# An attention result divided with its features on partitions, its row sums moved by DMA

## The chip, the cores and the metric

The kernel runs on one core of a Trainium2 chip. The core has five engines that run their own instruction streams in order: TensorE (PE in the profile; its weight loads are listed apart as PEld), VectorE (DVE), ScalarE (ACT), GpSimd (POOL) and SyncE (SP), which here only starts transfers. Engines wait for one another through semaphores. SBUF is the on-chip memory with 128 partitions; PSUM is the small memory that TensorE writes its products to.

The metric is the device time of one execution in microseconds (us). Lower is better. Before the change it was 1411.76 us, the median of three runs from 1406.98 to 1413.27.

## The reference

The kernel computes one decoder layer with post-normalisation, all in float32, on `x` of shape (16, 512, 256):

```
q = x@wq + 4*(x@Aq)@Bq ;  k = x@wk ;  v = x@wv + 4*(x@Av)@Bv      # 16 heads of 16 features
q, k = rope(q), rope(k)
a = softmax(causal(q k^T / 4)) @ v                                 # per head, 512 x 512 scores
x1 = layernorm(x + a @ wo)                                         # no scale, no shift
h  = gelu(butterfly_up(x1 @ W_exp + b_exp) + up_bias)              # 1024 hidden features
y  = layernorm(x1 + butterfly_down(h) @ W_con + b_con + down_bias)
```

A butterfly is ten stages of 2x2 mixes between features whose numbers differ in one bit. It is linear, so the kernel folds both butterflies into the two weight matrices at run time, on the chip, during the first batches.

## The kernel before

There are 16 batches (`B`) of 512 tokens, 4 token tiles of 128 (`NT`), 256 features in 2 chunks of 128 (`NC`), and 1024 hidden features in 8 chunks (`NHC`).

**Attention.** Scores are computed with keys on partitions, so the softmax can't take a row maximum along the free axis. Each batch is therefore gone through twice. `largest` computes q k^T with queries on partitions, and VectorE reduces each product to the row maximum (line 427); `place_largest` transposes these and puts them into a spare row of q. `weights` computes the scores again, transposed, with the maximum already subtracted by that spare row; ScalarE takes the exponential out of PSUM (line 487), and GpSimd zeroes the masked half of each diagonal block (line 491). `weigh` multiplies by v (line 514). The operand `vaug` holds 32 columns for each head, 16 of v and 16 of ones, so the 32 output rows of a head are 16 result features and 16 copies of the sum of the exponentials. Four heads fill the 128 partitions of the PSUM tile `po`: the even or the odd heads (`par`) of one chunk (`c`). One such pass, (b, c, par), is a quad here; a batch has four.

**Dividing and turning.** `normalize_heads` copies `po` to SBUF on ScalarE (line 529). `turn_back` transposes it on TensorE in four pieces, tokens to partitions (line 536); VectorE takes the reciprocals of the sums (line 539) and multiplies (line 541). When all four quads of a batch are done, `turn_heads` transposes each token tile back, features to partitions (line 552), ScalarE copies it out of PSUM (line 554), and `project_out` multiplies by `wo` (line 561), adds x on VectorE (line 565) and takes the statistics of the first layer norm (lines 575, 576).

**Behind it.** `spread` adds epsilon (line 587) and takes the power -1/2 on GpSimd (line 588). `offset` makes the shift on VectorE (line 593), `centre` applies both on ScalarE, one instruction for each token tile (line 600), and `turn_x1` transposes the normalised tile for the next product (line 614). `hidden` is the product with the folded up-weights (line 631), copied out of PSUM alternately by VectorE and ScalarE; `gelus` follows on ScalarE, `contract` is the product with the folded down-weights (line 658) in two halves for each token tile. Then come `spread`, `offset` and `centre` of the second layer norm and `store`.

**Order.** No scheduler reorders anything: the order of the program is the order on each engine. It is written as a loop over slots. A batch takes 20 slots (`per`), a quad 5 (`PER_QUAD`), and the `weights` pass runs 15 slots behind the `largest` pass (`behind`). In each slot come first the score products of both passes, then the work on them (exponentials, masks, the VectorE reductions), then the `weigh` step that is due, then the list `others[slot]`, then `holes[slot]`, then pieces of the folding of the weights. `add(s + n, f, ...)` puts a function into `others` of the slot n after the first slot s = 20 b of batch b. The lists are filled batch by batch, so within a slot the older batch's functions stand first. Since a batch's work reaches 64 slots past its start, a slot holds work of up to four batches. The prediction calls a slot by its number modulo 20: p4 is slot 4 of every twenty, and within a quad u0 to u4 are the slots modulo 5.

The score products of a slot go to two PSUM tiles, `pb` and `pa`, of which there is one each, so the products of a slot wait for the exponentials and reductions of the slot before. In u0 to u3 one of the two tiles belongs to `weights` and the other to `largest`; in u4 each holds half of both. All other products share a ring of three PSUM tiles.

## Time and profile before

| | |
|---|---|
| time, median of three runs | 1411.76 us (1406.98 to 1413.27) |
| the profiled execution | 1415.53 us, its span in the trace 1413.8 us |
| instructions | 24605 |
| VectorE, ScalarE, GpSimd busy | 59%, 51%, 36% of the span |
| DMA, mean over the span | 36 GB/s |
| transposes for dividing and turning | 256 of `oT`, 128 of `o` |
| `wo` products | 256 instructions |
| VectorE reductions of `largest` | 1024, with a read of the accumulator each |
| GpSimd masks | 512 |

Busy times of a group are the union of its instructions' times. TensorE's instructions overlap each other, so the sum of its groups is more than its busy time; the chain of work that ended last gives the share in which an instruction was not overlapped by the one before. A float32 product with moving data appears as two instructions in the trace and a transpose as one. In a list of instructions each line has the start, the duration, the engine, the line, the operation, output and input, and in brackets how long the engine had been idle before it and what ended that.

### The profile page before, as it was taken

How to read it: one execution, taken by the hardware profiler on the slowest of the kernel's cores; microseconds unless marked ns; L12 is line 12 of the kernel's file. 1: busy time of each engine (PE TensorE's matmuls, PEld its weight loads, DVE VectorE, ACT ScalarE, POOL GpSimd, SP SyncE). 2: the span in 40 equal slices, each digit the busy share in tenths (PEclk: the TensorE clock that was granted, in tenths of full speed). 3: DMA queues.
4: the chain of work that ended last, by engine and by line, in shares of the span. 5: the costliest groups of instructions: out<-in, count | busy, mean ns of one | idle time of the engine just before them, and what ended most of it. 6: DMA issues, size and time to landing. Idle time of an engine off the chain costs nothing.

```text
span 1413.8 us, 24605 instructions
## 1 busy us (share of the span) xinstructions
PE 1379.7 (98%) x9208; PEld 758.6 (54%) x9208; DVE 828.0 (59%) x2846; ACT 720.1 (51%) x1120; POOL 511.0 (36%) x779
## 2 busy tenths in 40 slices
PE   8899999999999999999999999999999999998998
PEld 4454546465564645555464555545455564644565
DVE  5766656556575655657465565746556574664422
ACT  2665455544555454555445455544545555445553
POOL 3534225253342425334252433514244252521311
PEclk9998999999999999999999999999999999999999
DMA  5310000100010010001101100010011001000000
GB/s 180 114 31 16 32 31 16 61 17 32 31 47 30 17 53 24 32 31 32 46 17 42 36 32 31 23 55 16 32 46 32 31 17 60 3 31 2 16 1 30
DMA packets 36472, 50.43 MB, mean 36 GB/s; under 512 B 3704, under 2 KB 23160, under 8 KB 36352
## 3 DMA queue, kind: packets, MB, share of 16 engines
q1 hardware_dynamic: 32464, 43.30, 8.8%
q10 hardware_dynamic: 3888, 5.55, 1.3%
q8 instruction: 73, 1.20, 0.3%
q14 instruction: 47, 0.39, 0.1%
HBM read 22.88 MB, written 8.39 MB: 22 GB/s over the span
## 4 chain that ended last, share of the span: by engine, by line
PE 94%; ACT 2%; DVE 2%; issue 1%; DMA 0%; POOLq 0%; POOL 0%; DVEq 0%; ACTq 0%
PE pb L470 20%; PE py L658 17%; PE ph L631 16%; PE po L514 11%; PE pqk L339 8%; PE pwo L561 4%; PE pvv L385 4%; PE pa L418 3%; PE pto L536 2%; PE pb L418 2%; DVE junk L427 1%; PE ptm L443 1%; PE pt L614 1%; PE ptc L552 1%; PE pd L269 1%; PE pa L470 1%
## 5 line engine op out<-in xcount | busy, mean ns | idle before, releaser
L427 DVE CUSTOM_DVE_ANT_0 junk<-pa,causal 128x384 bf16<-128x384 f32 (+2 forms) x878 | 439.3, 500 | 240.9 <-PE pa L418 209.5
L487 ACT ACTIVATE pT<-pb 128x1024 f32<-128x1024 f32 (+1 forms) x314 | 293.7, 935 | 365.4 <-PE pa L418 266.6
L491 POOL TENSOR_SCALAR_AFFINE_SELECT pT<-pT 128x256 f32<-128x256 f32 x512 | 202.5, 408 | 755.6 <-ACT pT L487 751.3
L470 PE MATMUL pb<-qz,kz 17*128 17x512 f32 (+2 forms) x1756 | 330.0, 475 | 10.7 <-ACT pT L487 9.9
L418 PE MATMUL pa<-kz,qz 32*128 32x384 f32 (+3 forms) x1756 | 324.6, 469 | 3.8 <-DVE mx L427 3.7
L658 PE MATMUL py<-wdn,h 128*128 128x256 f32 x1024 | 253.3, 392 | 1.4 <-ACT h L649 1.4
L631 PE MATMUL ph<-x1T,yb 128*128 128x512 f32 x512 | 236.1, 605 | 0.0
L470 PEld LDWEIGHTS pb<-qz,kz 17*128 17x128 f32 (+1 forms) x1756 | 142.3, 184 | 154.7 <-issue 92.7
L658 PEld LDWEIGHTS py<-wdn,h 128*128 128x128 f32 x1024 | 185.2, 190 | 69.6 <-issue 43.7
L514 PE MATMUL po<-pT,vaug 128*32 128x512 f32 (+3 forms) x2048 | 179.7, 446 | 0.0
L418 PEld LDWEIGHTS pa<-kz,qz 32*128 32x128 f32 (+1 forms) x1756 | 148.7, 185 | 18.5 <-DVE mx L427 9.9
L631 PEld LDWEIGHTS ph<-x1T,yb 128*128 128x128 f32 x512 | 92.4, 190 | 115.3 <-issue 101.7
L427 DVE CUSTOM_DVE_ANT_0 junk<-pb,causal 128x256 bf16<-128x256 f32 (+3 forms) x146 | 63.6, 435 | 111.2 <-ACT pT L487 102.2
L339 PE MATMUL pqk<-xT,wqk 128*128 128x512 f32 x256 | 119.4, 617 | 0.0
L644 ACT COPY h<-ph 128x512 f32<-128x512 f32 x57 | 33.4, 585 | 147.2 <-PE ph L631 147.2
L514 PEld LDWEIGHTS po<-pT,vaug 128*32 128x32 f32 x2048 | 47.4, 109 | 103.2 <-issue 89.4
L427 DVE DVE_READ_ACCUMULATOR2_ANT mx<- 128x1 f32 x1024 | 84.8, 83 | 0.0
L339 PEld LDWEIGHTS pqk<-xT,wqk 128*128 128x128 f32 x256 | 48.6, 197 | 67.1 <-issue 55.2
L600 ACT ACTIVATE z<-z,norm 128x256 f32<-128x256 f32 x128 | 66.9, 590 | 27.6 <-DVE norm L593 27.6
L367 POOL TENSOR_TENSOR swap<-swap,rope_sb 128x512 f32<-128x512 f32 x62 | 79.8, 1287 | 0.0
L588 POOL TENSOR_TENSOR norm<-norm,power 128x4 f32<-128x4 f32 (+1 forms) x38 | 35.0, 922 | 113.7 <-DVE norm L587 111.7
L649 ACT ACTIVATE h<-h,hbias 128x512 f32<-128x512 f32 x115 | 72.0, 708 | 0.2
(96 smaller groups left out, 1419.4 us busy)
## 6 DMA issues: line engine op xcount, KB each, us to landing
xT<-in_xT SPq DMA_DIRECT2D x16, 512.0 KB
swap<-qz SPq DMA_DIRECT2D x64, 128.0 KB
swap<-kz SPq DMA_DIRECT2D x64, 128.0 KB
z<-in_x SPq DMA_DIRECT2D x16, 512.0 KB
out_y<-z SPq DMA_DIRECT2D x15, 512.0 KB
early<-in_wexpT ACTq DMA_DIRECT2D x1, 1028.0 KB
wdn<-in_wcon ACTq DMA_DIRECT2D x1, 1024.0 KB
qz<-mT SPq DMA_DIRECT2D x64, 8.0 KB
```

The lines of the kernel that those rows point to most:

```text
L339: nc.tensor.matmul(pq, wqk[:, d, e : e + P], xTs[b][:, d, :], start=(d == 0), stop=(d == NC - 1))
L367: engine.tensor_tensor(swap, swap, rope_sb[:, 1, :], ALU.mult)
L418: lambda i=i, rows=rows, at=at, n=n, t=t, ps=ps: nc.tensor.matmul(ps[:, i, at : at + n], q[rows, par, t * P : n], k_[rows, par, 0:n], star ...
L427: lambda i=i, at=at, n=n, t=t, col=col, ps=ps: nc.vector.tensor_tensor_reduce(out=junk[:, 0:n], in0=ps[:, i, at : at + n], in1=causal[:, T ...
L470: lambda i=i, rows=rows, at=at, n=n, k=block, ps=ps: nc.tensor.matmul(ps[:, i, at : at + n], kt[rows, par, k * P : (k + 1) * P], qt[rows, ...
L487: nc.scalar.activation(pT[:, heads, 0:n], ps[:, :, at : at + n], AF.Exp)
L491: nc.gpsimd.affine_select(out=diag, in_=diag, pattern=[[0, 2], [1, P]], compare_op=ALU.is_ge, fill=0.0, base=0, channel_multiplier=-1,)
L514: nc.tensor.matmul(po[HG * g : HG * (g + 1), k * P : T], vaugs[b % 2][:, k, h, :], pT[:, g, at : at + n], start=(k == 0), stop=(group == 2),)
L600: nc.scalar.activation(zs[b][:, t, :], zs[b][:, t, :], AF.Identity, bias=norm[:, 2, t : t + 1], scale=norm[:, 1, t : t + 1],)
L631: nc.tensor.matmul(ph, wup[:, c, hc * P : (hc + 1) * P], state["x1T", b][:, c, :], start=(c == 0), stop=(c == NC - 1),)
L649: nc.scalar.activation(h[:, hc, :], h[:, hc, :], AF.Gelu, bias=hbias[:, hc : hc + 1])
L658: nc.tensor.matmul(py, state["h", b][:, hc, t * P : (t + 1) * P], wdn[:, hc, :], start=(hc == 0), stop=(hc == NHC - 1),)
```

## The change

The result of `weigh` stays with features on partitions. `vaug` is laid out for each pair of heads with ones at every even column and the two heads' features, interleaved, at every odd one. Read from column 33 it gives v, 1, v, 1, ... for the even head, read from column 0 it gives 1, v, 1, v, ... for the odd head. So the even head's features land on even partitions with its sums on the odd ones, and the odd head's the other way round. `wv`, `Bv` and `wo` are permuted on the host to match. After the ScalarE copy to SBUF, transfers on SP's queue, of 64 partitions each, put the sums beside the features they belong to: for an even quad one transfer to `sums`, for an odd quad one to `sums` and one that drops its features between those of the even quad. `normalize` then takes, for each chunk and token tile, the reciprocal of 128x128 sums in place on VectorE and multiplies 128x128. `project_out` reads the result directly. `turn_back`, `turn_heads` and the copy of `ocT` are gone.

Four other things change. `project_out` and what follows it stand three slots later, and the slots of `project_v`, the projections, `load_x`, `hidden` and `contract` are set anew. The last stage of the up-butterfly runs as products with diagonal matrices on TensorE instead of multiply-adds on ScalarE and VectorE. VectorE copies two of the eight hidden chunks out of PSUM instead of four, and ScalarE the others. The fillings of `vaug` and `mx` stand at the start of the program.

```diff
--- before.py
+++ after.py
@@ -181,7 +181,7 @@
         qz.append([const.tile([P, 2, T], F32, name=f"qz{r}_{c}") for c in range(NC)])
         kz.append([const.tile([P, 2, T], F32, name=f"kz{r}_{c}") for c in range(NC)])
     for r in range(2):
-        vaugs.append(const.tile([P, NT, NH, HG], F32, name=f"vaug{r}"))
+        vaugs.append(const.tile([P, NT, NH // 2, 2 * HG + 2], F32, name=f"vaug{r}"))
     for c in range(NC):
         mxs.append(const.tile([P, NT, P], F32, name=f"mx{c}"))
 
@@ -189,11 +189,10 @@
 
         return ap.rearrange("(g i) t -> g i t", i=HG)[:, first : first + count, :]
 
-    def prepare_mx(c):
+    for r in range(2):
+        nc.gpsimd.memset(vaugs[r], 1.0)
+    for c in range(NC):
         nc.gpsimd.memset(mxs[c], 0.0)
-
-    def prepare_vaug(r):
-        nc.gpsimd.memset(vaugs[r][:, :, :, DH:HG], 1.0)
 
 
 
@@ -281,7 +280,7 @@
         for s in stages:
             for c in range(NHC):
                 if not c & (1 << (s - NSP)):
-                    by = across_by_products if side == 0 and s < NS - 1 else across_chunks
+                    by = across_by_products if side == 0 else across_chunks
                     yield by(side, s, c, y, cols)
 
     def mixed(one, two):
@@ -389,7 +388,12 @@
                 start=(d == 0),
                 stop=(d == NC - 1),
             )
-        nc.scalar.copy(vaugs[b % 2][:, t, :, 0:DH], pv.rearrange("p (h i) -> p h i", i=DH))
+        nc.scalar.copy(
+            vaugs[b % 2][:, t, :, 1 : 1 + 2 * HG].rearrange("p g (h i e) -> p g h i e", h=2, e=2)[
+                :, :, :, :, 0
+            ],
+            pv.rearrange("p (g h i) -> p g h i", h=2, i=DH),
+        )
 
 
 
@@ -510,10 +514,10 @@
         for k in GROUPS[group]:
             n = width(k)
             for g in range(NG):
-                h = 2 * NG * c + 2 * g + par
+                first = 0 if par else HG + 1
                 nc.tensor.matmul(
                     po[HG * g : HG * (g + 1), k * P : T],
-                    vaugs[b % 2][:, k, h, :],
+                    vaugs[b % 2][:, k, NG * c + g, first : first + HG],
                     pT[:, g, at : at + n],
                     start=(k == 0),
                     stop=(group == 2),
@@ -522,44 +526,39 @@
         if group == 2:
             normalize_heads(b, c, par, po)
 
+
+
+
+    def rows_of(ap, e):
+        return ap.rearrange("(i two) t -> i two t", two=2)[:, e, :]
+
     def normalize_heads(b, c, par, po):
-        if (c, par) == (0, 0):
-            state["o", b] = ring2.tile([P, NT, NH, DH], F32, tag="o", name=f"o_{b}", bufs=1)
-        oT = ring2.tile([P, T], F32, tag="oT", name=f"oT_{b}_{c}_{par}")
-        nc.scalar.copy(oT, po)
-        state["back", b, c, par] = oT
-
-    def turn_back(b, c, par):
-        oT = state.pop(("back", b, c, par))
-        pt = bank(f"pto_{b}_{c}_{par}", [P, NT, P])
-        for t in range(NT):
-            nc.tensor.transpose(pt[:, t, :], oT[:, t * P : (t + 1) * P], ident)
-        heads = pt.rearrange("p t (g i) -> p t g i", i=HG)
-        rec = small.tile([P, NT, NG, 1], F32, tag="rec", name=f"rec_{b}_{c}_{par}")
-        nc.vector.reciprocal(rec, heads[:, :, :, DH : DH + 1])
-        o = state["o", b].rearrange("p t (c g two) i -> p t c g two i", c=NC, two=2)
-        nc.vector.tensor_tensor(
-            o[:, :, c, :, par, :],
-            heads[:, :, :, 0:DH],
-            rec.to_broadcast([P, NT, NG, DH]),
-            ALU.mult,
-        )
-
-    def turn_heads(b, t):
-        of = state["o", b][:, t, :, :].rearrange("p h i -> p (h i)")
-        pc = bank(f"ptc_{b}_{t}", [P, NC, P])
-        for c in range(NC):
-            nc.tensor.transpose(pc[:, c, :], of[:, c * P : (c + 1) * P], ident)
-        ocT = small.tile([P, NC, P], F32, tag="ocT", name=f"ocT_{b}_{t}", bufs=4)
-        nc.scalar.copy(ocT, pc)
-        state["ocT", b, t] = ocT
+        x = ring2.tile([P, T], F32, tag=f"x{par}", name=f"x_{b}_{c}_{par}", bufs=1 if par else 3)
+        nc.scalar.copy(x, po)
+        if par == 0:
+            sums = ring2.tile([P, T], F32, tag="sums", name=f"sums_{b}_{c}")
+            state["heads", b, c] = x, sums
+            nc.sync.dma_start(rows_of(sums, 0), rows_of(x, 1))
+        else:
+            even, sums = state["heads", b, c]
+            nc.sync.dma_start(rows_of(sums, 1), rows_of(x, 0))
+            nc.sync.dma_start(rows_of(even, 1), rows_of(x, 1))
+
+    def normalize(b, c, t):
+        x, sums = state["heads", b, c]
+        ts = slice(t * P, (t + 1) * P)
+        nc.vector.reciprocal(sums[:, ts], sums[:, ts])
+        nc.vector.tensor_tensor(x[:, ts], x[:, ts], sums[:, ts], ALU.mult)
 
     def project_out(b, t):
-        ocT = state.pop(("ocT", b, t))
         pw = bank(f"pwo_{b}_{t}", [P, D])
         for c in range(NC):
             nc.tensor.matmul(
-                pw, ocT[:, c, :], wo_sb[:, c, :], start=(c == 0), stop=(c == NC - 1)
+                pw,
+                state["heads", b, c][0][:, t * P : (t + 1) * P],
+                wo_sb[:, c, :],
+                start=(c == 0),
+                stop=(c == NC - 1),
             )
         z = zs[b]
         nc.vector.tensor_add(z[:, t, :], pw, z[:, t, :])
@@ -638,7 +637,7 @@
         h = state["h", b][:, hc, :]
         if fused:
             nc.scalar.activation(h, ph, AF.Gelu, bias=hbias[:, hc : hc + 1])
-        elif hc % 2 == 0:
+        elif hc % 4 == 0:
             nc.vector.tensor_copy(h, ph)
         else:
             nc.scalar.copy(h, ph)
@@ -707,20 +706,17 @@
         add((-2, -1, 0, 0)[t], project_v, 0, t)
     for n, at in enumerate((-1, 4, 6, 9, 12)):
         add(at, load_more, n)
-    for i in range(2):
-        add(-head, prepare_mx, i)
-        add(4 + i, prepare_vaug, i)
     for b in range(B):
         s = b * per
         if b > 0:
 
-            at = {1: (-16, -11, -13, -9), B - 1: (-4, 7, 7, 11)}.get(b, (-4, -3, 14, 11))
+            at = {1: (-16, -11, -13, -9), B - 1: (-3, 10, 10, 11)}.get(b, (-3, 4, 11, 11))
             for t in range(NT):
                 add(s + at[t], project_v, b, t)
         if b + 1 < B:
 
             add(s - head * (b == 0), load_xT, b + 1)
-            at = {0: (2, 5, 7, 10), 1: (3, 6, 8, 11)}.get(b, (7, 7, 7, 7))
+            at = {0: (2, 5, 7, 10), 1: (3, 6, 8, 11)}.get(b, (10, 10, 10, 10))
             for i, (c, side) in enumerate(chains):
                 holes.setdefault(s + at[i], []).append(
                     lambda b=b, side=side, c=c: start_projection(b + 1, side, c)
@@ -729,40 +725,39 @@
                     add(s + max(at[0] + 1 + 3 * i, at[i] + 1) + step, turn, b + 1, side, c, step)
                 for step in range(1 + side):
                     add(s + max(at[0] + 1 + 3 * i, at[i] + 1) + 4 + step, part, b + 1, side, c, step)
-        add(s + 5, load_x, b)
+        add(s + 9, load_x, b)
         add(s + 11, place_largest, b, 0)
         add(s + 21, place_largest, b, 1)
-        for n in range(NQ):
-            at = s + behind + PER_QUAD * n + 6 + (b + 1 == B)
-            if at < end:
-                add(at, turn_back, b, n // 2, n % 2)
+        for c in range(NC if b + 1 < B else 1):
+            for t in range(NT):
+                at = s + ((26, 27, 28, 29), (36, 37, 38, 40))[c][t] + (b + 1 == B)
+                add(at, normalize, b, c, t)
         if b + 1 < B:
             for t in range(NT):
-                add(s + (37, 37, 37, 38)[t], turn_heads, b, t)
-                add(s + (38, 38, 39, 39)[t], project_out, b, t)
-            add(s + 39, spread, 1, b)
-            add(s + 40, offset, 1, b)
-            add(s + 41, centre, 1, b)
+                add(s + 41 + t // 2, project_out, b, t)
+            add(s + 42, spread, 1, b)
+            add(s + 43, offset, 1, b)
+            add(s + 44, centre, 1, b)
             for c in range(NC):
-                add(s + 42, turn_x1, b, c)
+                add(s + 45, turn_x1, b, c)
         if b + 2 < B:
             for hc in range(NHC):
-                add(s + 43 + hc // 2, hidden, b, hc)
-            holes.setdefault(s + 47, []).insert(0, lambda b=b: gelus(b))
+                add(s + 46 + hc // 2, hidden, b, hc)
+            holes.setdefault(s + 50, []).insert(0, lambda b=b: gelus(b))
             for t in range(NT):
                 for half in range(2):
-                    at = (8, 9, 10, 12, 13, 15, 20, 21)[2 * t + half]
+                    at = (12, 13, 14, 15, 16, 18, 20, 23)[2 * t + half]
                     add(s + 40 + at, contract, b, t, half)
-            add(s + 61, spread, 2, b)
-            add(s + 62, offset, 2, b)
-            add(s + 62, centre, 2, b)
-            add(s + 62, store, b)
+            add(s + 63, spread, 2, b)
+            add(s + 64, offset, 2, b)
+            add(s + 64, centre, 2, b)
+            add(s + 64, store, b)
 
 
 
     y, z = B - 2, B - 1
     edge = B * per
-    for hc, at in enumerate((3, 6, 8)):
+    for hc, at in enumerate((6, 7, 8)):
         add(edge + at, hidden, y, hc)
     add(edge + 10, gelus, y, 3)
     for hc, at in ((3, 10), (4, 10), (5, 10), (6, 11), (7, 11)):
@@ -771,10 +766,10 @@
     add(end - 3, contract, y, 0, 0)
     add(end - 1, contract, y, 0, 1)
     add(end + 2, contract, y, 1, 0)
-    add(end + 2, turn_back, z, NC - 1, 1)
     add(end + 2, contract, y, 1, 1)
     for t in range(NT):
-        add(end + 2, turn_heads, z, t)
+        add(end + 2, normalize, z, NC - 1, t)
+    add(end + 2, contract, y, 2, 0)
     for t in range(NT + 1):
         if t < NT:
             add(end + 3, project_out, z, t)
@@ -782,7 +777,6 @@
         if t > 0:
             add(end + 3, offset, 1, z, t - 1, t)
             add(end + 3, centre, 1, z, t - 1, t)
-    add(end + 3, contract, y, 2, 0)
     add(end + 3, contract, y, 2, 1)
     add(end + 3, contract, y, 3, 0)
     for c in range(NC):
@@ -803,8 +797,8 @@
     first, second = fold_tasks()
     fold = first + second
     tasks_at = dict(zip(range(2, behind), (0, 1, 2, 3, 4, 4, 5, 5, 5, 6, 9, 11, 14)))
-    for s in range(behind, 2 * per + 3):
-        tasks_at[s] = len(first) + -(-len(second) * (s - behind + 1) // (2 * per + 3 - behind))
+    for s in range(behind, 2 * per + 5):
+        tasks_at[s] = len(first) + -(-len(second) * (s - behind + 1) // (2 * per + 5 - behind))
     ahead = 0
     given = 0
     due = deque()
@@ -933,14 +927,17 @@
     attn = {k[len("L0_attn_") :]: v for k, v in given.items() if k.startswith("L0_attn_")}
     ffn = {k[len("L0_ffn_") :]: v for k, v in given.items() if k.startswith("L0_ffn_")}
     x = attn["query"]
+
+    by_pair = np.arange(x.shape[-1]).reshape(-1, 2, DH)[:, ::-1].reshape(-1)
+    by_dim = np.arange(x.shape[-1]).reshape(-1, 2, DH).transpose(0, 2, 1).reshape(-1)
     feeds = {
         "x": x,
         "xT": x.transpose(0, 2, 1),
         "wq": attn["wq"],
         "wk": attn["wk"],
-        "wv": attn["wv"],
-        "wo": attn["wo"],
-        "lora": np.stack([attn["Aq"].T, attn["Bq"], attn["Av"].T, attn["Bv"]], axis=1),
+        "wv": attn["wv"][:, by_pair],
+        "wo": attn["wo"][by_dim],
+        "lora": np.stack([attn["Aq"].T, attn["Bq"], attn["Av"].T, attn["Bv"][:, by_pair]], axis=1),
         "wexpT": np.concatenate([ffn["W_exp"].T, ffn["b_exp"][:, None]], axis=1),
         "coef": np.stack(
             [
```

## The prediction

> **What bounds the kernel now.** I read the page's busy table first, then the chain of work that ended last, then the costs by line.

> ```profile
> PE 1379.7 (98%) x9208; PEld 758.6 (54%) x9208; DVE 828.0 (59%) x2846; ACT 720.1 (51%) x1120; POOL 511.0 (36%) x779
> PE 94%; ACT 2%; DVE 2%; issue 1%; DMA 0%; POOLq 0%; POOL 0%; DVEq 0%; ACTq 0%
> L536 PE MATMUL pto<-ident,oT 128*128 128x128 f32 x256 | 40.7, 282 | 0.0
> L552 PE MATMUL ptc<-ident,o 128*128 128x128 f32 x128 | 20.1, 280 | 0.2 <-DVE z L666 0.2
> L539 DVE RECIPROCAL rec<-pto 128x16 f32<-128x16 f32 x64 | 16.2, 254 | 44.2 <-PE pto L536 44.2
> L600 ACT ACTIVATE z<-z,norm 128x256 f32<-128x256 f32 x128 | 66.9, 590 | 27.6 <-DVE norm L593 27.6
> ```

> TensorE is the bound; a batch of twenty slots takes 82.6 us from 224 to 1215 us. Any new wait of TensorE therefore counts in full. The lists in order of time, from p1 (its products start at 658.22) to p4 (669.92), show how ScalarE keeps up:

> ```profile
> 659.40 1.02 ACT L487 ACTIVATE pT<-pb 128x1024 f32<-128x1024 f32 x1 [2.00 <-PE pa L418]
> 660.32 2.06 ACT L600 ACTIVATE z<-z,norm 128x256 f32<-128x256 f32 x4
> ...
> 665.36 2.08 ACT L600 ACTIVATE z<-z,norm 128x256 f32<-128x256 f32 x4 [0.89 <-DVE norm L593]
> 667.34 1.00 ACT L487 ACTIVATE pT<-pb 128x1024 f32<-128x1024 f32 x1
> ```

> The centring of the first norm (660.32) and that of the second (665.36) stand in different slots. The second waits for the shift on VectorE and pushes p3's exponential to 667.34. TensorE doesn't notice, because p3 has 3.63 us of `hidden` behind its scores. The chain in the same stretch, and two slots before it a place where TensorE does notice VectorE:

> ```profile
> 636.50 1.06 PE pb L470 x4
> 637.56 0.71 PE pa L418 x4
> ...
> 664.24 1.02 PE pt L614 x8
> ...
> 666.36 3.63 PE ph L631 x8
> ```

> At 636.50 the u4 slot before had only 2.1 us behind its scores. VectorE's reductions of `pa` ended at 636.98, so `pb` and `pa` ran one after the other, 1.77 us for a usual 1.07.

> **Removed.** In the chain four `oT` transposes take 0.44 or 0.59 us: 64 groups at 0.515 are 33.0. Eight `o` transposes take 1.03 (0.81+0.22): 16 batches, 16.5. Together -49.5 us on the bound. The `ocT` copies (20.7 us of ScalarE) and VectorE's old multiply (27.2) were hidden; they count only as room.

> **Added on TensorE.** One more butterfly stage: 32 instructions of 128x257. Eight of 128x256 take 1.92, so 7.7 us; the windows to 142 us show 14 us of idle TensorE there, so some of it is covered. Bounds 0 and 7.7; I take +5.

> **Normalising on VectorE.** 128 steps, each a reciprocal and a multiply of 128x128. The trace has only a reciprocal of 128x16, 253 ns. If a column costs what the multiply rows show (692-425 ns for 256 columns, 1.04 ns), 128 columns take 0.37 us. If all above the 0.16 us that those rows leave as a fixed part is per column, it is 5.9 ns each: 0.92 us. A 128x4 scalar operation takes 0.17, so the fixed part isn't much less, and 0.97 is the upper end. I take 0.92, since the excess of 95 ns over the fixed part needs an explanation and columns are the plain one. The multiply is 0.158+0.133 = 0.29.

> Both inputs of the multiply now lie in SBUF; before, one lay in PSUM. The row that bears on this: `offset`, a VectorE operation on two SBUF inputs, takes 0.24 us by median, and 1.11 us from 657.93 while GpSimd multiplied from 657.75 to 659.01. GpSimd has a 1.27 us operation in each slot p11 to p2, in a slot of some 3 us, so such a multiply waits about 1.27²/2/3 = 0.27 us; a step is 1.5 us there.

> [...]

> **Transfers.** 96 of 128 KB on SP, at 0.54 us of issue each. SP is nearly always waiting, and its waits for ScalarE's mT copies alone are 557 us. Behind a transfer that waits for the ScalarE copy stand only later slots' transfers; POOL's queue issues none. Landing isn't shown. The last store's data were ready at 1411.25 and the span ends at 1413.8: under 2.6. At the start, beside the weight loads, a swap issued to 36.9 was waited for until 41.87: 5. I take 2.6. The copy ends 2.7 us into p15 (as at 619.04), so sums land 5.3 and features 5.9 us in, where VectorE reaches the step 6.1 us in: hidden, with 0.2 to 0.8 us to spare.

> **Moved.** The swaps go with their projections from p7 to p10, the load of x from p5 to p9, the store (512 KB) from p2 to p4. None is issued in p11 to p15. The store stands on SP just ahead of the transfers of p5; if these come late, VectorE waits in p6, where it needs 3.3 us of a slot of 4.8, and `hidden` covers TensorE. `gelus` moves with the projections, whose 7.07 us of products cover it (ScalarE 7.6) as they do now. `contract` and `project_v` keep their counts; where they stand decides A and B.

> **Hidden edits.** `hidden` copies moved to ScalarE (0.585 each) lie in p6 to p9, where TensorE works 4.7 to 5.8 us a slot. The fillings lie before 20.0 us, where GpSimd waits 14.6 us for the first swap. The strided v copy has the same 256 columns. Without that cover the copies cost 0.6 us each.

> **New wait A, p4 to p6.** The first norm's `centre` moves from p1 to p4, `offset` and `centre` of the second from p2 to p4, `turn_x1` from p2 to p5. Both centrings now share a slot, the older batch's first, and that one needs `offset`, which stands behind p4's reductions. From p4's start: reductions begin at 1.8 (633.25 to 635.05) and last 1.93; `offset` ends at 4.0; four centrings take 2.08, to 6.1; the other four, to 8.15. `turn_x1` needs the last of these and ends at 8.9. On ScalarE the kz copy (0.72), v copy (0.37) and p5's exponential (1.0) follow, to 10.25, and only then may p6's scores start. By TensorE's own work they would start at 1.2+1.0+1.0 (p4) + 1.07+0.57+1.02 (p5) = 5.9. Loss 4.4 us, for 13 slots p4 (those with both centrings): +57. Bounds: nothing, if TensorE is late anyway, and 5.5, if VectorE comes a microsecond late into p4.

> **New wait B, p19 to p0.** p19 now has no `others` work on TensorE. From p15's start: VectorE's step at p16 ends at 7.6, p17's reductions at 9.5 and step at 11.0, p18's reductions at 12.9, the residual add and statistics at 13.9, step at 15.4, p19's reductions at 17.3 (the `pb` half 16.4). TensorE could start p0 at 14.9; it runs `pb` from 16.4 and `pa` to 18.1, where 15.9 was possible: 2.2 us, as at 636.50 but worse. 14 times, +31. With a 0.37 us reciprocal it is 1.5; with VectorE free, still 1.2 for the empty slot; the upper end is 3.

> **Sum.** Against the profiled execution's 1415.5: -49.5 +5 +57 +31, -4 for the old kernel's own losses (82.6 less 82.3 us of work a batch, 13 batches), +1 for the tail, where four steps of 1.2 us replace 1.3 us of transposes beside `contract`: 1456. That execution was 3.8 above the median of the runs, so **1452**.

> **Rivals.**
> - Wait A doesn't form: 1452-57 = 1395, faster. It decides below (57-40.5)/13 = 1.3 us a batch. For it: ScalarE is 51% busy and hid the same centring at 665.36. Against it: that needed 3.63 us of `hidden`, and p5 has only `turn_x1`, which waits for the same engine.
> - Neither wait forms and the whole saving stays: 1364. Against it: 636.50 shows wait B already.
> - Wait A is half: TensorE, late from B, absorbs some; 1.3 to 3 us a batch give 1412 to 1434.
> - Transfers land late: at the 5 us of the start VectorE stands 2.4 us at p16, with the reductions behind it and TensorE behind those: 14 times, 1486. Against it: the queue moves little in p11 to p15.

> **How the numbers follow.** Forecast 0.62 (1434 to 1472 by the bounds of A, B and the reciprocal), A half 0.10, A gone 0.16, both gone 0.04, late transfers 0.08. A measurement tells about 0.5% (7 us). Half of "A half" and 0.01 of "A gone" lie within it: same 0.06, faster 0.19, slower 0.75. The range 1396 to 1478 leaves out both gone, half of A gone and most of the late transfers.

> **What would show it.** Right: in p5 TensorE idle before `turn_x1`, ended by ScalarE's z; p6's scores released by pT; in p0 `pa` released by VectorE's maxima; a 128x128 reciprocal near 0.92 us; VectorE not waiting for DMA. The prediction is wrong if `centre` runs early in p4, or if TensorE is near 98% busy without idle time at `turn_x1`.

## The result and the profile after

The changed kernel takes 1494.47 us, the median of four runs from 1493.33 to 1500.70. The kernel before, run beside it, takes 1412.51 us (1406.98 to 1415.47). The ratio is 1.0593, with a 95% interval from 1.0560 to 1.0627. The profiled execution took 1493.33 us with a span of 1491.6 us, which is 77.8 us more than the span of before. The prediction was 1452 us, so the direction was right and the loss was twice as large as forecast (82 us against 40). Of one kernel below (the second norm two slots later) three of ten runs, above 1424 us, count as slow: its ratio leaves them out, its median holds them.

From the page of the changed kernel come the busy table, the chain, and three groups of instructions with their busy time, mean ns of one, and idle time before them:

```profile
PE 1411.2 (95%) x8856; PEld 743.0 (50%) x8856; DVE 908.8 (61%) x2937; ACT 721.5 (48%) x1101; POOL 512.7 (34%) x779
PE 84%; ACT 8%; DVE 5%; issue 2%; DMA 0%; POOL 0%; ACTq 0%; POOLq 0%; DVEq 0%
L550 DVE RECIPROCAL sums<-sums 128x128 f32<-128x128 f32 x128 | 120.7, 943 | 0.0
L599 ACT ACTIVATE z<-z,norm 128x256 f32<-128x256 f32 x128 | 65.5, 588 | 46.7 <-DVE norm L592 46.7
...
L630 PE MATMUL ph<-x1T,yb 128*128 128x512 f32 x512 | 260.5, 657 | 0.0
```

TensorE has 352 instructions fewer and is busy for 31.5 us longer. That can't be added work. Its share of the chain fell from 94% to 84%, and ScalarE and VectorE took what it lost. The list of ScalarE's instructions in order of time, from p4's centrings to p5's exponential, shows the first wait:

```profile
696.14 4.04 ACT L599 ACTIVATE z<-z,norm 128x256 f32<-128x256 f32 x8 [1.60 <-DVE norm L592]
700.09 0.80 ACT L379 ACTIVATE kz<-kz,lead,odd 128x512 f32<-128x512 f32 x1
700.79 0.37 ACT L391 COPY vaug<-pvv 128x256 f32<-128x256 f32 x1
701.05 1.01 ACT L491 ACTIVATE pT<-pb 128x1024 f32<-128x1024 f32 x1
```

All eight centrings stand in one block. They start when VectorE's `offset` (L592) is done, and the kz copy, the v copy and the exponential of p5 stand behind them. TensorE's list shows what that does, and before it the place where p19 meets p0:

```profile
676.93 1.13 PE L474 MATMUL pb<-qz,kz 32*128 32x512 f32 x4 [1.09 <-issue]
678.02 1.13 PE L422 MATMUL pa<-kz,qz 16*128 16x512 f32 x4
...
698.76 0.33 PE L613 MATMUL pt<-ident,z 128*128 128x128 f32 x1 [0.89 <-ACT z L599]
...
702.12 1.22 PE L474 MATMUL pb<-qz,kz 17*128 17x512 f32 x2 [1.12 <-ACT pT L491]
...
704.13 6.07 PE L630 MATMUL ph<-x1T,yb 128*128 128x512 f32 x8
...
712.21 3.70 PE L630 MATMUL ph<-x1T,yb 128*128 128x512 f32 x8
```

Wait A is at 698.76 (TensorE waits for the centring) and at 702.12 (it waits for p5's exponential). Wait B is at 676.93, where `pb` is late by 1.09 and `pa` runs after it and not with it. The last two lines are what the prediction doesn't have: eight `hidden` products take 6.07 us right after wait A, and the same eight take 3.70 us one slot later. The table of stretches of 10 us around the wait of another batch gives the reason. Its columns are the stretch, its length, the busy time of PE, PEld, DVE, ACT and POOL with their instructions, the granted TensorE clock, the DMA share and GB/s:

```profile
1130.00:1140.00 10.00, 8.88 (x78) 5.00 (x70) 7.14 (x30) 5.62 (x11) 4.72 (x7) 1.00 0.05 18
1140.00:1150.00 10.00, 8.63 (x22) 3.56 (x22) 4.35 (x9) 3.90 (x7) 3.12 (x3) 0.66 0.35 117
1150.00:1160.00 10.00, 10.00 (x57) 4.35 (x56) 5.52 (x21) 3.80 (x5) 1.53 (x4) 1.00 0.00 1
```

The granted clock is 0.66 in the stretch behind the wait and 1.00 around it. TensorE pays for wait A twice: it idles, and then it runs slowly.

To see where the 77.8 us lie, both traces can be laid side by side at the same slots, by the `weigh` products of u4 (16 in a row). Slot 64 is p4 of the batch in which both centrings meet for the first time, slot 304 the same place twelve batches later:

| stretch | before | after | difference | in the prediction |
|---|---|---|---|---|
| start to slot 64 | 254.4 | 252.8 | -1.6 | +0.1 |
| slots 64 to 304, twelve batches | 998.9 | 1061.7 | +62.8 | +38.4 |
| slot 304 to the end | 160.5 | 177.1 | +16.6 | +2.0 |
| sum | 1413.8 | 1491.6 | +77.8 | +40.5 |

The last column distributes the prediction's terms: three batches' transposes (-9.3), the butterfly stage (+5) and two waits B (+4.4) to slot 64; in each of the twelve batches -3.1 for transposes, -0.3 for the old losses, +4.4 and +2.2 for the waits; the rest behind slot 304.

Behind slot 304 the largest piece is one slot wide. The chain of the changed kernel there:

```profile
1401.48 0.44 DVE z L665
...
1402.87 1.02 POOL norm L587
...
1403.91 0.36 DVE norm L592
...
1404.80 3.54 ACT z L599 x7
...
1408.39 1.10 PE pt L613 x5
```

Here, with no later batch's work left to run beside it, a whole norm lies open: residual sum, statistics, the power on GpSimd, the shift, the centrings, and only then `turn_x1`, 6.9 us from 1401.46 to 1408.39. The stretch from slot 324 to 329 grows from 9.87 to 17.48 us.

### The profile page after: what moved, and what is told of

The parts are those of the page before. It is cut to its first block, busy times and chain, and to the rows that moved or that the text cites. A ratio compares the mean times of both kernels' runs of the same rounds, so it can differ in the third digit from the quotient of the medians.

```text
span 1491.6 us, 24052 instructions
## 1 busy us (share of the span) xinstructions
PE 1411.2 (95%) x8856; PEld 743.0 (50%) x8856; DVE 908.8 (61%) x2937; ACT 721.5 (48%) x1101; POOL 512.7 (34%) x779
## 4 chain that ended last, share of the span: by engine, by line
PE 84%; ACT 8%; DVE 5%; issue 2%; DMA 0%; POOL 0%; ACTq 0%; POOLq 0%; DVEq 0%
PE pb L474 19%; PE ph L630 17%; PE py L657 16%; PE po L518 8%; PE pqk L338 7%; PE pwo L556 4%; ACT z L599 4%; DVE junk L431 3%; PE pvv L384 3%; PE pa L422 3%; ACT pT L491 3%; PE pb L422 1%; PE pd L268 1%; PE pa L474 1%; PE ptm L447 1%
## 5 line engine op out<-in xcount | busy, mean ns | idle before, releaser
L474 PE MATMUL pb<-qz,kz 17*128 17x512 f32 (+2 forms) x1756 | 342.2, 489 | 42.3 <-ACT pT L491 25.3
L422 PE MATMUL pa<-kz,qz 32*128 32x384 f32 (+3 forms) x1756 | 337.5, 484 | 3.8 <-DVE mx L431 3.7
L630 PE MATMUL ph<-x1T,yb 128*128 128x512 f32 x512 | 260.5, 657 | 0.0
L657 PE MATMUL py<-wdn,h 128*128 128x256 f32 x1024 | 256.8, 396 | 0.0
L474 PEld LDWEIGHTS pb<-qz,kz 17*128 17x128 f32 (+1 forms) x1756 | 145.5, 188 | 202.7 <-issue 113.6
L630 PEld LDWEIGHTS ph<-x1T,yb 128*128 128x128 f32 x512 | 102.0, 210 | 147.6 <-issue 128.5
L643 ACT COPY h<-ph 128x512 f32<-128x512 f32 x86 | 50.3, 585 | 181.1 <-PE ph L630 181.1
L550 DVE RECIPROCAL sums<-sums 128x128 f32<-128x128 f32 x128 | 120.7, 943 | 0.0
```

What stands on the lines that cost most here:

```text
L422: lambda i=i, rows=rows, at=at, n=n, t=t, ps=ps: nc.tensor.matmul(ps[:, i, at : at + n], q[rows, par, t * P : n], k_[rows, par, 0:n], star ...
L474: lambda i=i, rows=rows, at=at, n=n, k=block, ps=ps: nc.tensor.matmul(ps[:, i, at : at + n], kt[rows, par, k * P : (k + 1) * P], qt[rows, ...
L550: nc.vector.reciprocal(sums[:, ts], sums[:, ts])
L630: nc.tensor.matmul(ph, wup[:, c, hc * P : (hc + 1) * P], state["x1T", b][:, c, :], start=(c == 0), stop=(c == NC - 1),)
L657: nc.tensor.matmul(py, state["h", b][:, hc, t * P : (t + 1) * P], wdn[:, hc, :], start=(hc == 0), stop=(hc == NHC - 1),)
```

## The experiments

Every kernel was compared with the kernel before, run beside it. That kernel's medians in the three groups of runs were 1413.92, 1415.36 and 1414.04 us, so ratios are compared, and the microseconds beside them are close to comparable. "Period" is the time from the first `wo` product of a batch to that of the next, as a mean of eleven batches of the profiled execution. It is 83.32 us before the change and 88.16 us after.

| kernel | median, us | ratio to before (95%) | period, us |
|---|---|---|---|
| before | 1412.51 | 1 | 83.32 |
| after | 1494.47 | 1.0593 (1.0560 to 1.0627) | 88.16 |
| second norm two slots later | 1411.12 | 0.9952 (0.9918 to 0.9986) | 83.23 |
| wait A partly filled | 1468.18 | 1.0387 (1.0371 to 1.0402) | 86.36 |
| reciprocal of 16 columns | 1472.03 | 1.0412 (1.0393 to 1.0431) | 87.48 |
| p18's down product to p19 | 1504.20 | 1.0653 (1.0619 to 1.0686) | 89.62 |
| second norm later, a v tile to p19 | 1399.03 | 0.9892 (0.9868 to 0.9915) | 81.37 |
| old result in the new slots | 1539.10 | 1.0886 (1.0858 to 1.0914) | 92.09 |
| second norm later, last stage as before | 1409.90 | 0.9968 (0.9946 to 0.9990) | 82.19 |
| second norm later, p0's down product to p19 | 1387.23 | 0.9828 (0.9800 to 0.9857) | 81.10 |
| second norm later, two steps later | 1431.28 | 1.0140 (1.0104 to 1.0175) | 83.84 |
| the last two together | 1403.58 | 0.9936 (0.9913 to 0.9958) | 82.16 |

### Wait A taken away: the second norm two slots later

```diff
-            add(s + 64, offset, 2, b)
-            add(s + 64, centre, 2, b)
-            add(s + 64, store, b)
+            add(s + 66, offset, 2, b)
+            add(s + 66, centre, 2, b)
+            add(s + 66, store, b)
```

> Only the shift, the centring and the store of the second norm stand two slots later (p6 instead of p4), so the first norm's centring is alone in p4. Theory 1 (ScalarE's order and the clock that falls after it): in the changed kernel TensorE loses 3.96 us from p4 to p6 (9.83 us from 692.29 to 702.12 for 5.87 us of its own work) and then up to 3.4 us in p6, where the same products took 6.00 instead of 3.63 us and the scores 2.06 instead of 1.04. Both go: a batch falls from 88.1 to some 82 us, 12 batches and the end give -80, about 1415 us, and the granted clock is back near 0.99. Rival 2 (VectorE's longer work is the cost): VectorE has as much to do as before, so less than 10 us is gained. Rival 3 (the clock falls because the transposes are gone, not because of the wait): the wait goes but the clock stays at 0.96, about -48, 1446 us.

Three lines give 83 us back by the medians (90 by the ratios). The four centrings of the first norm now have p4 for themselves, and the first pair of `hidden` products takes 3.63 us in the chain (3.70 in a list) in every batch, so the slow products behind wait A went with the wait. From the lists of ScalarE and TensorE, at p4 and p6 of one batch:

```profile
675.16 2.07 ACT L599 ACTIVATE z<-z,norm 128x256 f32<-128x256 f32 x4
...
680.63 3.70 PE L630 MATMUL ph<-x1T,yb 128*128 128x512 f32 x8
```

The chain of this kernel around wait B in two batches:

```profile
317.16 1.04 issue
318.20 1.13 PE pb L474 x4
...
321.86 3.71 PE py L657 x8
...
657.66 1.13 PE pb L474 x4
...
660.45 1.92 PE py L657 x8
```

The wait is 1.04 us in both. Behind the first the down products take 3.71 us, behind the second 1.92. Stretches laid at the times at which the clock changes show the granted clock (the third number from the right):

```profile
316.44:319.85 3.41, 2.32 (x24) 0.86 (x16) 2.45 (x10) 1.14 (x3) 2.05 (x3) 1.00 0.00 0
319.85:326.67 6.82, 6.82 (x28) 3.24 (x24) 2.56 (x6) 1.18 (x2) 1.65 (x2) 0.50 0.28 95
...
654.36:657.77 3.41, 2.32 (x35) 1.36 (x35) 3.11 (x12) 1.08 (x2) 2.70 (x4) 1.00 0.01 2
657.77:664.60 6.83, 6.83 (x38) 3.52 (x39) 4.38 (x13) 2.73 (x4) 2.23 (x4) 1.00 0.23 78
```

So the same wait costs 1.8 us more on the down products alone, and 3.2 us a batch, in some batches than in others. The batches with the slow products are the ones with the long periods: 85.28, 85.27, 85.28, 83.65, then 82.05 for most. The runs differ in the same way: one of 1402.97 us has a mean granted clock of 0.990, one of 1421.14 us has 0.978.

### Is the slow clock caused by the idle time? Wait A partly filled

```diff
+    def fill(b, count):
+        pf = bank(f"pf_{b}_{count}", [P, T])
+        for d in range(count):
+            nc.tensor.matmul(
+                pf, wqk[:, d, 0:P], rope_sb[:, 0, :], start=(d == 0), stop=(d == count - 1)
+            )
...
+            add(s + 45, fill, b, 2)
             for c in range(NC):
                 add(s + 45, turn_x1, b, c)
+            add(s + 45, fill, b, 1)
```

> The wait stays and TensorE gets extra products that nothing reads in p5: four instructions of 128x512 ahead of the transposes of the normalised tile, two behind them, about 1.7 and 0.9 us, which fit into the idle time of the changed kernel (0.9 us before the first transpose, gaps between the transposes, 1.1 us before p6's scores). Theory 1: the granted clock doesn't fall, the first pair of hidden products takes 3.63 us, p6's scores start when they did: 2.4 to 3.4 us a batch less in the batches in which it fell, -30 to -40 us, about 1458 us, though the wait itself is untouched. Rival 3 (the clock falls for another reason): the clock stays at 0.96 and the time at 1494 or up to 20 us above.

`fill` runs products of 128x512 whose result nobody reads, four instructions ahead of `turn_x1` and two behind it. The chain of this kernel in p4 to p6 of one batch:

```profile
691.46 3.04 ACT z L599 x6
...
698.12 3.63 PE ph L637 x8
```

ScalarE's block is what it was (3.04 for the last six centrings, as in the changed kernel's chain at 697.14), so wait A stands. The first `hidden` pair takes 3.63 us in place of 6.00, in every batch. The time falls by 26 us to 1468.18, where 30 to 40 were expected. The clock behind wait A therefore costs at least 26 us or 2.2 in each of twelve batches, and it is caused by TensorE's idle time and not by something else that happens in p6. It is at least that much because `fill` has a price of its own: from p4's scores to p6's it takes 10.45 us, by the starts in the lists, where the changed kernel takes 9.90. Periods of 85.9 us in nine of twelve batches and 87.5 to 87.9 in three say that a slow clock is still met elsewhere: it is behind wait B, where the granted clock is 0.50 for 3.4 us three times (once from 586.50 to 589.91).

### VectorE's load: the reciprocal of 16 columns

```diff
-        nc.vector.reciprocal(sums[:, ts], sums[:, ts])
+        few = slice(t * P, t * P + 16)
+        nc.vector.reciprocal(sums[:, few], sums[:, few])
```

> The reciprocal is taken of 16 of the 128 columns of each token tile; the other 112 columns are multiplied by the plain sums, so the result is another one. 128 instructions shrink from 0.94 to about 0.25 us, 88 us less work for VectorE. Theory 1: VectorE is late in one place only (p16 to p0), where the 2.2 us go to about 1.4; 14 times, -10 us, about 1484. Rival 2 (VectorE's longer work is the cost): up to -88 us, about 1410.

The median is 1472.03. The reciprocals fall from 120.7 to 31.2 us, while the multiplies rise from 45.2 to 62.0, so VectorE is relieved of 73 us. TensorE's chain at wait B and at the first `hidden` pair:

```profile
667.03 0.54 issue
667.57 1.13 PE pb L474 x4
668.70 1.09 PE pa L422 x4
...
694.85 5.56 PE ph L631 x8
```

Wait B falls only from 1.04 to 0.54 of idle time, and `pb` and `pa` still run one after the other. Wait A and the slow products stay. So the division on VectorE as such, which was the rival, isn't what makes the kernel slow: 73 us less of it gave 22 us. That is twice the 10 expected; about half of it comes from two batches, 5.4 us each, in which the clock fell behind wait B in the changed kernel and doesn't here.

### What is wait B made of? Work for p19, from three places

```diff
-                    at = (12, 13, 14, 15, 16, 18, 20, 23)[2 * t + half]
+                    at = (12, 13, 14, 15, 16, 19, 20, 23)[2 * t + half]
```

> One half of the product with the down-weights moves from p18 to p19, where TensorE has nothing but scores and the product with v. Theory 1: p0's scores no longer wait (they started 1.0 us late and ran 1.13+1.09 instead of 1.07 us), 2.2 us a batch, 14 times, about -28 us, 1466 us; the wait in p4 to p6 stays. Rival 2 (VectorE's longer work is the cost): VectorE has the same work in the same stretch, and the time stays within 10 us of 1494.

This was a miss: 10 us slower than the changed kernel. The chain shows that p0 no longer waits, but that p19 does:

```profile
673.41 0.47 DVE junk L431
...
675.21 0.48 PE pa L474 x2
...
676.46 1.87 PE po L518 x16
678.33 2.53 PE py L657 x8
```

p18 has lost its 1.92 us, so p19's scores wait for p18's reductions, and behind that wait the `weigh` products take 1.87 us for a usual 1.00. The reading "p19 has no work" was too narrow. In the changed kernel VectorE works without a pause from 668.66 to 677.87, from p17 to the reductions of p19. It is late as a whole, and moving TensorE's work within that stretch only moves the wait.

The next kernel brings work into p19 from outside that stretch, on top of the later second norm:

```diff
-            at = {1: (-16, -11, -13, -9), B - 1: (-3, 10, 10, 11)}.get(b, (-3, 4, 11, 11))
+            at = {1: (-16, -11, -13, -9), B - 1: (-3, 10, 10, 11)}.get(b, (-3, 4, -1, 11))
```

> On top of the run with the second norm two slots later, one product with the v weights moves from p11 to p19 of the slots before its batch, so that TensorE has 1.0 us more behind p19's scores and loses no cover elsewhere in p16 to p18. (The move of half a down-weight product from p18 to p19 gave +10 us instead of -28: it only moved the wait to p19's own scores, where pa waited for p18's reductions until 675.21, 2 us.) Theory 1b: from p16 to p0 VectorE has 12.6 us of work in a row and TensorE 11.3; 1 us of the 2.2 us loss goes, and with the shorter idle time the clock falls less often (it fell in p0 in about half the batches of that run, 3.2 us each): -14 to -35 us, 1376 to 1397. If the empty slot alone were the cause, all of the loss would go, -40, near 1370. If the loss is only moved again: 1411 or above.

1399.03 us, 12 less than with the later second norm alone by the medians and 8 by the ratios. The idle time at p0 is 0.03 us in the chain, `pb` (1.13) and `pa` (1.09) still run one after the other, and no batch has slow products there: eleven periods lie between 81.35 and 81.48. The median lies 2 us above the upper end of the expectation, and why isn't shown. The profiled execution (1404.48 us) is 5.5 above that median and lost about as much at its start: the granted clock up to 70 us is 0.88, where the kernel with the later second norm had 0.98, and slot 19 comes at 75.5 in place of 70.0 us.

Then the first half of the last down product, moved from p0 to p19, which leaves p16 to p18 as they are:

```diff
-                    at = (12, 13, 14, 15, 16, 18, 20, 23)[2 * t + half]
+                    at = (12, 13, 14, 15, 16, 18, 19, 23)[2 * t + half]
```

> The kernel with the second norm two slots later, and the last token tile's first half of the down product in p19 instead of p0, so p16 to p18 keep all their TensorE work. Theory: p19's 1.92 cover VectorE's excess of 1.04, and p0 loses them: there the next scores wait for one exponential (about 1.0) and for VectorE's reductions, against 0.57 of the weigh step, so 0.5 to 1.5 come back in p0. Net gain 0.7 to 1.7 a batch and up to 1.8 of clock in three to five batches: 1380 to 1405. If the wait only moves to p0 in full: 1404 to 1418.

1387.23 us, within the expectation and the best of all: 1.7% faster than the kernel before (0.9800 to 0.9857 of its time). A half product of 1.92 us cost 10 us when it came from p18, and gave 24 us by the medians (18 by the ratios) when it came from p0. TensorE's list at p19 to p1:

```profile
637.71 1.99 PE L657 MATMUL py<-wdn,h 128*128 128x256 f32 x8
639.64 0.70 PE L474 MATMUL pb<-qz,kz 32*128 32x512 f32 x2
...
641.02 0.64 PE L518 MATMUL po<-pT,vaug 128*32 128x256 f32 x8
641.95 1.13 PE L474 MATMUL pb<-qz,kz 32*128 32x512 f32 x4 [0.29 <-ACT pT L491]
```

p0's scores follow p19's product at once, and 0.29 us of waiting come back at p1. Eleven periods lie between 81.09 and 81.20, and the four runs between 1386.45 and 1388.47.

The last kernel of this group relieves VectorE in place of giving TensorE work. The third and fourth step of the second chunk move from p18 and p0 to p0 and p1:

```diff
-                at = s + ((26, 27, 28, 29), (36, 37, 38, 40))[c][t] + (b + 1 == B)
+                at = s + ((26, 27, 28, 29), (36, 37, 40, 41))[c][t] + (b + 1 == B)
```

> The kernel with the second norm two slots later, and of the second chunk's four steps (reciprocal and multiply) the third stands in p0 instead of p18 and the fourth in p1 instead of p0. Theory (wait B is the sum of VectorE's work from p16 to p0): in the trace of that kernel VectorE works without a pause up to 658.5, with a step of 1.28 at 655.42 ahead of p19's reductions, and then idles 1.31 and 1.00 in p0 and p1. With the step moved there, p19's reductions end 1.3 earlier, the idle 1.04 ahead of pb is gone and about 1.1 of the serial pb and pa stays; the clock doesn't fall behind it. 14 times 1.04, and 1.8 of clock in three to five batches: 19 to 24 us, 1387 to 1396. Rival (the empty slot alone makes the wait, whatever VectorE does): no change within 0.5%, 1404 to 1418.

Another miss, by 35 us: 1431.28, slower than without the edit. A line of VectorE's list at p19, and behind it TensorE's list in p0 and p1:

```profile
652.80 0.42 DVE L431 CUSTOM_DVE_ANT_0 junk<-pb,causal 128x256 bf16<-128x256 f32 x1 [0.66 <-ACT pT L491]
```

```profile
653.80 1.13 PE L474 MATMUL pb<-qz,kz 32*128 32x512 f32 x4 [0.59 <-ACT pT L491]
...
659.51 1.99 PE L556 MATMUL pwo<-wo_sb,x 128*128 128x256 f32 x8
662.88 0.66 PE L447 MATMUL ptm<-ident,mx 128*128 128x128 f32 x4 [1.38 <-DVE z L564]
```

VectorE now has 0.66 us to spare, and then waits for p19's exponential on the tile that, in u4, holds work for both engines. Of the 1.09 us that the list of the changed kernel has at p0, 0.59 stay, and the exponential ends them: that part of the cost of the empty slot stays though VectorE has time to spare. The step that moved to p1 stands ahead of the residual sums of `project_out`, and those free the ring of PSUM tiles that the transposes of `mx` need: a new wait of 1.38 us at 662.88. Both edits together:

> Both edits together: VectorE's excess is gone and p19 has work, but p0 now has two reductions, a step and no down product. By theory p19 to p0 then run without idle and with pb and pa together (2.2 gained), p0 loses 0.5 to 2: 1375 to 1400. If p0's step makes the wait there, 1400 to 1420.

1403.58 us, in the second of the two ranges. The wait that the moved steps make is in p1 again: TensorE waits 0.60 us for the exponential there and then 1.26 for the residual sum, with or without work in p19.

### The slots without the divided result

The kernel before, with the slots of the changed kernel for `project_out` and everything behind it, `project_v`, the projections, `load_x` and the end of the folding. Dividing and turning are the old ones:

```diff
-                add(s + (38, 38, 39, 39)[t], project_out, b, t)
+                add(s + 41 + t // 2, project_out, b, t)
...
-            add(s + 41, centre, 1, b)
+            add(s + 44, centre, 1, b)
...
-            add(s + 62, centre, 2, b)
+            add(s + 64, centre, 2, b)
```

> The kernel before, with its transposes and without any of the new transfers and 128x128 reciprocals, but with the slots of the changed kernel: output projection, norms, transposes of the normalised tile, hidden products and products with the down-weights where the changed kernel has them; the projections, v tiles and the load of x too. Theory 1 (the slots are the cause, above all both centrings in p4): the batch of 83.3 us gains the 4 us of the wait and the 2.5 to 3 us of the slower clock in p6, and about 1 us for the empty p19: 12 to 13 batches, 1480 to 1510 us. Rival (the divided result itself, by VectorE's load and the transfers, is the cause): within 15 us of 1412.

1539.10 us, above the expected range. Moving alone costs 124 us over the kernel before; the divided result in the same slots gives 45 of them back by the medians (1539.10 to 1494.47; 41 by the ratios), close to the 49.5 us of transposes. The two kernels also differ in the size of their waits and in where the clock falls, so that agreement is in part luck. TensorE's chain has the same two waits and the same slow products behind them:

```profile
692.81 0.54 issue
693.34 1.13 PE pb L470 x4
...
696.13 3.61 PE py L658 x8
...
717.54 3.04 ACT z L600 x6
...
722.51 1.22 PE pb L470 x2
...
724.60 4.76 PE ph L631 x8
```

So neither the transfers nor the reciprocals are needed for the loss. What the expectation missed is again the clock (3.61 in place of 1.92, 4.76 in place of 3.63), and here also waits of the old transposes for the copy of `ocT` (0.46 us before 704.07).

### The last butterfly stage

On top of the later second norm, the last stage of the up-butterfly as multiply-adds on ScalarE and VectorE, as before the change:

```diff
-                    by = across_by_products if side == 0 else across_chunks
+                    by = across_by_products if side == 0 and s < NS - 1 else across_chunks
```

> The run with the second norm two slots later, but the last stage of the up-butterfly as multiply-adds on ScalarE and VectorE, as before the change. It measures one edit that the prediction put at +5 us between 0 and 7.7: 32 products less on TensorE, 8 multiply-adds of about 0.7 us more on VectorE and 8 of 0.5 us on ScalarE while the weights are folded. Expected 1411 less 5, between 1403 and 1414.

1409.90 against 1411.12 us, ratios 0.9968 and 0.9952 with overlapping intervals: no difference that these runs can tell. The +5 of the prediction is neither confirmed nor refuted.

## Why the prediction was wrong

**Bound and removed work: right.** TensorE was the bound, and the transposes were worth what their chain pieces say: -49.5 by the prediction, -41 to -45 between the old result in the new slots and the changed kernel, which differ in the divided result, the butterfly stage and the hidden copies, and in waits: the old result waits 0.46 us a batch for `ocT`, and 0.54 in place of 1.04 at wait B. The size is confirmed to some 10 us, not better.

**Reciprocal and multiply: right.** The 128x128 reciprocal takes 943 ns by mean (0.92 taken), and none of the 128 takes more than 0.95 us (0.97 was the upper end). The multiply takes 353 ns by mean; while GpSimd multiplies (for example from 667.07 to 668.33 and from 670.49 to 671.76) it takes 0.49 and 0.51 us, and 0.29 where GpSimd does not (681.52). Both of the longer multiplies end 0.15 to 0.16 us after the GpSimd instruction does. The 0.27 us that the prediction added to each of four steps were too high: 0.20 and 0.22 in p16 and p17, 0.09 in p18, nothing in p0.

**Transfers: right.** Before the 128 reciprocals VectorE was idle for 0.0 us in all, before the multiplies for 4.5, so late transfers can't have cost more than that.

**Wait A: right in mechanism and size.** Predicted were 10.25 us from p4's scores to p6's for 5.9 of work, a loss of 4.4. Measured were 9.83 (692.29 to 702.12), a loss of 3.9, with each link as described: shift, eight centrings, kz copy, v copy, exponential. The experiment with the second norm shows that three lines of order hold it.

**Wait B: right in size, incomplete in cause.** 1.04 idle and 1.1 of `pb` and `pa` one after the other make the predicted 2.2. The upper end of 3 us is shown by no run: the idle time is 1.08 or 1.09 us in the lists at each of thirteen waits B of the changed kernel. The cause is VectorE's long stretch from p17 together with the empty slot. The prediction's statement that a free VectorE leaves part of it is borne out: 0.54 us of idle time in the chain stay both with the short reciprocal and with the moved steps, and 1.1 for `pb` and `pa` one after the other, 1.6 where 1.2 to 1.5 were predicted.

**The step that failed: the sum has no term for the granted clock.** It counts a wait as idle time and all of TensorE's instructions behind it at full speed. The first `hidden` pair behind wait A takes 4.4 to 6.1 us in place of 3.63, and in the batch shown p6's scores 2.06 (1.22 and 0.84 in the chain) in place of 1.04. The balance of a batch: the work without waits is 79.3 us (the period of the best kernel, 81.1, less 1.3 at p0 and p1 and 0.5 at p5, read off its trace). With 3.9 for A and 2.2 for B that makes 85.4, and twelve batches took 88.5 each: 3.1 a batch, 37 us in all. The granted clock places them: in these batches of the changed kernel it is 0.50 for 6.8 us behind every wait A (3.4 in one batch), and behind wait B only once, in the last (1296.04 to 1302.86). Filling wait A took 26 of the 37 away, which is shown. The other 11 are close to what the filled kernel itself loses: 5.3 in three batches whose clock falls behind wait B, and 6.6 for `fill`'s own products, 0.55 a batch. The trace of before had hardly shown the effect, since TensorE nowhere waited so long in its steady batches: its granted clock is 1.00 from 136 to 1282 us.

**The second step: "+1 tail".** Behind slot 304 the loss is 16.6 us where 2.0 were forecast. The moved norms meet there with nothing left to cover them: 7.6 us between slots 324 and 329, as shown above, and 5.6 between 304 and 314, where the prediction's 4.4 for the last wait A belong.

**A small one: the old kernel's losses.** The batch before takes 83.32 us and not 82.6; twelve batches between the same two slots take 998.9 us, and the stretch of 991 us that was read holds slightly less than twelve. Its losses are 83.32 - 3.1 - 79.3 = 0.9 a batch, where 0.3 were taken, which makes the prediction 8 us too high and hides a little of the missing clock.

**Rivals.** "A doesn't form" (1395) is close to what happens when it is taken away (1411). That it would form was decided rightly, by the length of ScalarE's queue behind `offset`.

## What to carry to other kernels

A change that saves work on the bound is worth its saving only in an order of work that still fits: here 45 us of saved transposes were outweighed by about 124 us of cost of the slots, and two small moves, the second norm out of the first norm's slot and one half product into the empty slot, brought the time from 1494 to 1387 us, below the 1412 of before. When two slots of a loop that overlaps batches are moved, list for each engine what stands in the same slot afterwards, older batches included. And price a wait of TensorE as its idle time plus a slower clock behind it; here the second part was half of the first.

## What the runs showed of the hardware that was not expected

**Short waits that let the clock fall.** In the changed kernel no single pause of TensorE around wait A is longer than 1.12 us; between 697.9 and 702.1 it idles 0.9, three times 0.16, and 1.1 us. Yet the clock behind it was 0.66 over a stretch of 10 us, and in it 0.50 for 6.83 us (702.12 to 708.95). At wait B the longest pause is 1.09 us, and with the old result in the new slots a pause of 0.54 us (692.81) was followed by down products of 3.61 us. Pauses of 0.54 to 1.12 us were thus followed by slow products, where the prediction had counted every product behind a wait at full speed.

**Run-to-run spread.** In the kernel with the second norm later, slower runs are those with a lower mean granted clock, as shown above, and the four runs of the best kernel lie within 2 us. But a wide spread isn't by itself a sign of long waits: the kernel before, whose clock is 1.00 from 136 to 1282 us of its trace, spreads from 1406.91 to 1420.37 us.
